# Moving the next chunk's first two gate steps between the transpositions of the first layer's chunks without fill

## The chip, the cores and the metric

The kernel runs on one core of one Trainium2 chip. The metric is the device time in microseconds of one launch, which covers all four layers of the network; the lower the better. A core has a matrix engine (TensorE, PE in the profile, with its weight loads as PEld), VectorE (DVE), ScalarE (ACT), GpSimd (POOL) and SyncE (SP, which here issues nearly all DMAs). Matrix products land in PSUM, from which VectorE and ScalarE copy them to SBUF.

## The reference

The input x has shape (8, 56, 56, 192). Four layers follow each other, each of the form x = x + layer(groupnorm(x)). Only layer 0, a gated convolution with Toeplitz matrices, is touched by the change:

```python
def _toeplitz(x, a):
    n = x.shape[1]
    m = 2 * n
    xf = jnp.fft.rfft(x, m, axis=1)
    af = jnp.fft.rfft(a, m, axis=0)
    return jnp.fft.irfft(xf * af[None], m, axis=1)[:, :n]
...
p = jax.nn.silu(x @ p_w.T + p_b)
q = jax.nn.silu(x @ q_w.T + q_b)
v = jax.nn.silu(x @ v_w.T + v_b)
...
qv = q * v
o1 = _toeplitz(qv.reshape(b * h, w, D1), a1).reshape(b, h, w, D1)
o2 = _toeplitz(jnp.transpose(qv, (0, 2, 1, 3)).reshape(b * w, h, D1), a2)
o2 = jnp.transpose(o2.reshape(b, w, h, D1), (0, 2, 1, 3))
out = p * (o1 + o2)
return out @ o_w.T + o_b
```

D1 is 576 channels, h and w are 56. a1 and a2 are small tables, one column per channel, computed once.

## The kernel before, in words

Layer 0 (`layer0`, from line 136) works image by image, b = 0 to 7, and within an image in five chunks c = 0 to 4 of its 576 channels. A chunk is two slabs of 64 channels (128 in all), but for the last, the tail, which is one slab. Everything is in 32-bit floats.

A chunk passes through three kinds of steps.

- **Gates and products** (`project`, line 283, four steps g = 0 to 3, each for a quarter of the image's rows). A step allocates PSUM tiles with `banks()` (tag "c", four slots of two banks each; a chunk of 128 channels needs two slots for q and v, the tail needs one), multiplies the normalized image by the weights on PE (L294 and L301), and evaluates SiLU twice on ScalarE into two SBUF tiles of the tag "s" (L310), of which there are four. `multiply` (line 316) then writes q times v into the one buffer `qv`, in two arrangements: a straight one on VectorE (L319) and a transposed one, mostly on GpSimd (L325, two instructions for each of g = 0 to 2; for g = 3 GpSimd and VectorE share it).
- **Turns** (`turn_both`, line 342, seven steps; `turn`, line 361, four steps for the tail). A step takes one PSUM slot, makes 16 transpositions of `qv` on PE (L352), and copies the result into the buffers ol and or (in the code `left` and `right`, for both slabs): the one half on VectorE, the other on ScalarE (L357). The copy on ScalarE begins when that on VectorE is done.
- **Convolutions** (`convolve`, line 382, two steps for a slab). A step takes one PSUM slot and makes 32 products of ol with or (L395), one channel each; the Toeplitz tables have been loaded by DMA into the other rows of ol and or. VectorE or ScalarE copies the result into `ot`. Behind a slab's last convolution `toeplitz` (line 265) has SP load the tables of the slab two further on, into the buffers that are free now. In image 0 these are built from small tables (`ed`) and stored to DRAM for the later images.

Every second chunk (c = 1 and 3) is followed by the output steps for two chunks (`post`, line 426): p, its SiLU (tag "s" too), transpositions of `ot`, products, and the output weights, added to `acca` and `accb`. The tail has the like in `post_tail`. They are kept as a list `fill` and run in the next chunk's turn phase.

The order of the work is written out in the loop from line 634. For a chunk c it is:

1. `merge(fill, turns)`: the chunk's turns, with the steps of `fill` in between. `fill` is the output of earlier chunks: of the tail of the image before for c = 0, of `post` for c = 2 and c = 4. It is empty for c = 1 and c = 3, and for c = 0 of image 0.
2. The next chunk's gates and products (`ahead`), merged with `beside`: in c = 0, 1 and 2 some steps of group norm (statistics of the image just finished, for the next layer, and the normalization of the next image). In c = 1 `beside` is `deviate` and `last` of `tell` (line 601), each with a small PE step (L98) between VectorE's.
3. The convolutions. In c = 3 (`c == NC - 2`) they alternate with the four tail gates of `ahead`.

`qv` exists once, so the next chunk's products must come behind this chunk's last turn, and the next chunk's turns behind all products.

TensorE's order is the order in which the code issues (line 627 puts PE under a manual schedule). The orders of the other engines are made by a planner that lists ready instructions by its own costs, earlier ones of the program first; the four slots of each tag are handed out in turn.

The merging rule spreads the shorter of two lists over the longer:

```python
def merge(a, b):
    n = max(len(a), len(b))
    for i in range(n):
        for x in (a, b):
            for f in x[-(-i * len(x) // n) : -(-(i + 1) * len(x) // n)]:
                f()
```

Of the kernel before, what the change touches and what calls it, by code (L numbers as in the profile page):

```python
# [73 lines left out]
def sub(ap, *dims):  # L74

    return bass.AP(ap.tensor, ap.offset, [list(ap.ap[0]), *(list(d) for d in dims)])
# [59 lines left out]
def layer0(cx, xin, xout, w, consts):  # L136
# [8 lines left out]
    NS, DS = 9, 64  # L145
# [5 lines left out]
    with ExitStack() as es:  # L151
# [7 lines left out]
        def banks():  # L159
            return cx.tile(psc, [128, 2, 512], "c")  # L160
# [104 lines left out]
        def toeplitz(n):  # L265

            b, s = divmod(n, NS)
            if b == B:
                return
            left, right = pairs[n % 2]  # L270
            sides = ((channels(right)[T2], T2), (channels(left)[T1], T1))
            if b:
                for d in (slice(d, d + 16) for d in range(0, DS, 16)):
                    for r, (dst, _) in enumerate(sides):
                        nc.sync.dma_start(dst[:, d], tables[s][r][:, d])
                return
            for r, (dst, _) in enumerate(sides):
                ed = eds[1 - r]
                src = bass.AP(ed.tensor, ed.offset + s * DS * NP, [[1, H], [NP, DS], [1, H]])
                nc.sync.dma_start(dst, src)  # L280
                nc.sync.dma_start(tables[s][r], dst)

        def project(xn, c):

            n = 7 * H
            tail = c == NC - 1
            js = [2 * c] if tail else [2 * c, 2 * c + 1]

            def step(g):
                pss = [banks() for _ in js]  # L290
                for j, ps in zip(js, pss):
                    for h in range(2):
                        at = h * HQ + g * n
                        nc.tensor.matmul(  # L294
                            ps[:, h, 0:n], wqv[0][:, j, :], xn[0][:, at : at + n],
                            start=True, stop=False,
                        )
                for j, ps in zip(js, pss):
                    for h in range(2):
                        rows = slice(h * CB, (h + 1) * CB)  # L300
                        nc.tensor.matmul(  # L301
                            ps[:, h, 0:n], wqv[1][rows, j, :], xn[1][rows, g * n : (g + 1) * n],
                            start=False, stop=True,
                        )
                ts = []
                for i in range(2):
                    j, ps = js[0 if tail else i], pss[0 if tail else i]
                    rows = slice(i * DS, (i + 1) * DS) if tail else slice(0, 128)
                    t = cx.tile(wk, [128, 2, n], "s")[0 : DS if tail else 128]
                    nc.scalar.activation(t, ps[rows, :, 0:n], AF.Silu, bias=bqv[rows, j : j + 1])  # L310
                    ts.append(t)
                multiply(g, slice(0, DS if tail else 128), ts)

            return [lambda g=g: step(g) for g in range(4)]

        def multiply(g, rows, ts):

            def straight():
                nc.vector.tensor_tensor(  # L319
                    sub(qv[rows, 7 * g :, 64 + H - 1 :], (HH * 120, 2), (120, 7), (-1, H)),  # L320
                    *(t.rearrange("p u (h w) -> p u h w", w=H) for t in ts), ALU.mult,
                )

            def across(eng, u, w0, w1):
                eng.tensor_tensor(  # L325
                    sub(qv[rows, w0:, H - 1 - 7 * g - HH * u :], (120, w1 - w0), (-1, 7)),
                    *(t[:, u].rearrange("p (h w) -> p w h", w=H)[:, w0:w1] for t in ts), ALU.mult,
                )

            if g < 3:  # L330
                straight()
                for u in range(2):
                    across(nc.gpsimd, u, 0, H)
                return

            for i, w in enumerate(((0, HH), (HH, H))):
                across(nc.gpsimd, 0, *w)
                across(nc.vector, 1, *w)
                if i == 0:
                    straight()  # L340

        def turn_both(n):

            order = (n % 2, 1 - n % 2)

            def step(i0):
                ps = banks()[0:120]
                view = ps.rearrange("p k (d i) -> p k d i", i=8)
                for i in range(8):
                    for e, k in enumerate(order):  # L350
                        rows = slice(e * DS, (e + 1) * DS)
                        nc.tensor.transpose(  # L352
                            view[:, k, :, i], qv[rows, i0 + i, :], ident[rows, rows]
                        )
                for t, rows, copy in zip(both, (T2, T1), (nc.vector.tensor_copy, nc.scalar.copy)):
                    dst = t[rows, :, 0:ND].rearrange("p k (d i) -> p k d i", i=H)
                    copy(dst[:, :, :, i0 : i0 + 8], view[rows])  # L357

            return [lambda i0=i0: step(i0) for i0 in range(0, H, 8)]

        def turn(n):

            s = n % NS
            e = s % 2 * DS
            left, right = pairs[n % 2]

            def step(i0, ni):
                ps = banks()[0:120]
                view = lambda k: ps[:, k].rearrange("p (d i) -> p d i", i=8)
                for i in range(ni):  # L370
                    nc.tensor.transpose(
                        view(i // 8)[:, :, i % 8], qv[e : e + DS, i0 + i, :],
                        ident[e : e + DS, e : e + DS],
                    )
                src = ps[:, 0 : ni // 8].rearrange("p k (d i) -> p d k i", i=8)
                for t, rows, copy in ((left, T2, nc.vector.tensor_copy), (right, T1, nc.scalar.copy)):
                    dst = channels(t)[rows, :, i0 : i0 + ni].rearrange("p d (k i) -> p d k i", i=8)
                    copy(dst, src[rows])

            return [lambda i0=i0: step(i0, min(16, H - i0)) for i0 in range(0, H, 16)]  # L380
# [233 lines left out]
# [7 lines that stand above are left out]
# [7 lines left out]
        xn, nxt = first, None  # L628
        merge(normalize(xn), [])
        for n in range(2):  # L630
            toeplitz(n)
        merge(project(xn, 0), [])
        fill, after, telling = [], None, []
        for b in range(B):
            more = b + 1 < B
            for c in range(NC):
                n = b * NS + 2 * c
                two = c < NC - 1
                turns = turn_both(n) if two else turn(n)
                merge(fill, turns)  # L640
                fill, beside = [], []
                if c == 0:
                    if after is not None:
                        image_dma(nc.sync, xout[b - 1], *after, store=True)
                        beside, telling = tell(b - 1, *after)
                    if more:
                        nxt = load_raw(b + 1)
                if c == 1:
                    acc = new_acc(b)
                    beside = [lambda f=f: f(bank) for f in telling]  # L650
                if c == 2 and more:
                    beside = normalize(nxt)

                if c % 2 == 0:
                    ot = cx.tile(cp, [120, 128, H] if two else [H, H, DS], "ot")
                ahead = project(xn, c + 1) if two else project(nxt, 0) if more else []
                convs = []
                for m in (n, n + 1) if two else (n,):
                    *some, last = convolve(m, ot)
                    convs += some + [lambda m=m, last=last: (last(), toeplitz(m + 2))]  # L660

                if c == NC - 2:
                    ahead = [f for pair in zip(ahead, convs[0:4]) for f in pair]
                    convs = convs[4:]
                merge(ahead, beside)
                for f in convs:
                    f()
                if c in (1, 3):
                    fill = post(c // 2, xn, ot, acc)
            fill, after = post_tail(xn, ot, acc), acc  # L670
            xn = nxt
# [1386 lines left out]
```

## Time and profile before

| | us |
|---|---|
| median of three runs | 4271.02 |
| lowest and highest of them | 4262.56, 4275.62 |
| the profiled execution's own time | 4265.11 |
| its span, first to last instruction | 4263.3 |
| granted TensorE clock, mean over the span | 0.971 |
| L352, matrix part: busy (3584 records) | 144.3 |
| L294, matrix part: busy (1152 records) | 435.9 |
| L310 on ACT: busy (320) | 278.2 |
| L357 on DVE and on ACT: busy (224 each) | 261.4 and 225.6 |
| L325 on POOL: busy (320) | 569.3 |

Times in the profile are microseconds from the first instruction of one execution. A line of the timeline reads: start, time busy, engine, source line, operation, tiles written and read, their sizes, and the number of instructions that were merged into the line; in brackets stands the idle time before it and what ended that. A matrix product in 32-bit floats can appear as more than one record, so the counts of L294, L301 and L395 are twice the code's. A line of the waits reads: engine, line, what it waited for, total, times, longest. A line of the stages reads: from and to, its length, then busy time and instructions of PE, PEld, DVE, ACT and POOL, the granted clock, the busy share of the DMA engines (slightly over 1 at times), and GB/s.

### The profile page before, as it was taken

What the parts mean: (1) busy time and instruction counts of PE and PEld (TensorE: products, weight loads), DVE (VectorE), ACT (ScalarE), POOL (GpSimd) and SP (SyncE); (2) the same over time, 40 slices, a digit from 0 to 9 for tenths busy, and PEclk for the clock granted to TensorE, in tenths of its full rate; (3) what the DMA queues carried; (4) which work ended last, traced back from release to release, by engine and by line L of the source; (5) the groups of instructions that cost most, each with busy time, mean ns of one, the idle gap of its engine ahead of it and who ended that gap; (6) DMA issues with size and microseconds to landing.
All of it is one profiled execution on the core that took longest, in us unless ns stands there. A gap on an engine that the chain in (4) does not pass through costs nothing.

```text
span 4263.3 us, 106441 instructions
## 1 busy us (share of the span) xinstructions
PE 3954.9 (93%) x46380; PEld 2553.1 (60%) x46380; DVE 2345.1 (55%) x3396; ACT 1781.1 (42%) x2020; POOL 1512.6 (35%) x1294
## 2 busy tenths in 40 slices
PE   6989999999999999999699999679998999998997
PEld 3666656666665656666366666434444555555997
DVE  4536565554656555464534444266666666664664
ACT  2434444334444433443233334133334555554664
POOL 3222232223223221332233333143334444444776
PEclk9999999999999999999799999889999999999999
DMA  6755242332524233241324444555547676664243
GB/s 142 141 106 145 62 114 71 81 86 62 145 62 115 74 81 84 62 122 47 92 75 107 97 105 108 146 153 169 166 141 186 167 166 162 151 156 112 73 115 94
DMA packets 379606, 484.13 MB, mean 114 GB/s; under 512 B 175780, under 2 KB 324372, under 8 KB 377236
## 3 DMA queue, kind: packets, MB, share of 16 engines
q1 hardware_dynamic: 373636, 466.97, 43.0%
q10 hardware_dynamic: 5504, 10.35, 0.8%
q8 instruction: 365, 5.98, 0.6%
q14 instruction: 101, 0.83, 0.1%
HBM read 321.49 MB, written 155.65 MB: 112 GB/s over the span
## 4 chain that ended last, share of the span: by engine, by line
PE 73%; DVE 7%; issue 7%; DMA 4%; SPq 3%; POOL 3%; ACT 2%; DVEq 0%; POOLq 0%; ACTq 0%
PE c L294 9%; PE v L1390 6%; PE c L395 6%; PE h L1892 5%; PE c L301 5%; PE c L481 4%; PE c L436 4%; PE c L943 4%; PE c L461 3%; PE y L978 3%; PE kv L1450 3%; PE c L443 3%; PE c L486 2%; DVE ol L357 2%; PE c L949 2%
## 5 line engine op out<-in xcount | busy, mean ns | idle before, releaser
L325 POOL TENSOR_TENSOR qv<-s,s 128x392 f32<-128x392 f32 (+3 forms) x320 | 569.3, 1799 | 1424.6 <-ACT s L310 1354.2
L294 PE MATMUL c<-xa,wqv 128*128 128x392 f32 x1152 | 435.9, 520 | 7.7 <-ACT or L357 4.8
L310 ACT ACTIVATE s<-c,bqv 128x784 f32<-128x784 f32 (+1 forms) x320 | 278.2, 910 | 389.9 <-PE c L301 232.8
L319 DVE TENSOR_TENSOR qv<-s,s 128x784 f32<-128x784 f32 (+1 forms) x160 | 190.4, 1190 | 268.2 <-ACT s L310 268.1
L357 ACT COPY or<-c 56x1024 f32<-56x1024 f32 x224 | 225.6, 1007 | 256.3 <-DVE ol L357 240.9
L294 PEld LDWEIGHTS c<-xa,wqv 128*128 128x128 f32 x1152 | 212.2, 196 | 177.2 <-issue 44.2
L395 PEld LDWEIGHTS c<-or,ol 120*64 120x64 f32 x9216 | 277.8, 138 | 55.7 <-issue 47.4
L395 PE MATMUL c<-or,ol 120*64 120x56 f32 x9216 | 287.2, 223 | 18.5 <-DMA ol<-ed 9.0
L357 DVE COPY ol<-c 56x1024 f32<-56x1024 f32 x224 | 261.4, 1208 | 63.4 <-PE c L352 63.4
L450 ACT ACTIVATE s<-c,bp 128x448 f32<-128x448 f32 x224 | 129.7, 630 | 271.0 <-PE c L443 271.0
L1390 PE MATMUL v<-wvb,wa 128*128 128x512 f32 (+1 forms) x400 | 192.6, 614 | 50.0 <-ACT wa L1301 30.7
L301 PE MATMUL c<-xb,wqv 64*128 64x392 f32 x1152 | 233.6, 519 | 0.0
L1923 POOL TENSOR_TENSOR y<-y,s 128x448 f32<-128x448 f32 x168 | 185.1, 1102 | 90.1 <-ACT s L1902 90.1
L1892 PE MATMUL h<-ringv,am 128*64 128x57 f32 (+1 forms) x4400 | 191.8, 235 | 18.3 <-DVE ringv L1879 11.3
L481 PE MATMUL c<-po,wo 128*128 128x448 f32 x448 | 198.1, 564 | 10.8 <-DVE po L470 10.8
L436 PE MATMUL c<-xa,wp 128*128 128x224 f32 x896 | 192.0, 358 | 3.2 <-issue 3.2
L1892 PE MATMUL h<-ringh,am 128*64 128x57 f32 (+1 forms) x4400 | 185.9, 231 | 8.0 <-DVE ringh L1898 7.8
L1401 ACT ACTIVATE vb<-sm 128x1024 f32<-128x1024 f32 (+1 forms) x100 | 103.7, 1038 | 211.2 <-issue 187.2
L424 DVE TENSOR_TENSOR acca<-c,acca 128x392 f32<-128x392 f32 (+1 forms) x120 | 67.3, 586 | 222.0 <-PE c L486 204.8
L352 PE MATMUL c<-ident,qv 64*120 64x64 f32 x3584 | 144.3, 227 | 44.2 <-ACT or L357 38.3
L1892 PEld LDWEIGHTS h<-ringv,am 128*64 128x64 f32 x4400 | 167.2, 140 | 21.5 <-DVE ringv L1879 12.2
L943 PE MATMUL c<-wv,xc 128*126 128x192 f32 x896 | 175.4, 339 | 0.7 <-DVE s L903 0.6
(224 smaller groups left out, 7690.6 us busy)
## 6 DMA issues: line engine op xcount, KB each, us to landing
or<-tt SPq DMA_DIRECT2D x252, 196.0 KB
ol<-tt SPq DMA_DIRECT2D x252, 196.0 KB
vt<-v SPq DMA_DIRECT2D x56, 672.0 KB
v<-vb SPq DMA_DIRECT2D x96, 384.0 KB
x<-x SPq DMA_DIRECT2D x112, 168.0 KB
x<-x SPq DMA_DIRECT2D x112, 112.0 KB
bt<-bs SPq DMA_DIRECT2D x28, 448.0 KB
bs<-bs SPq DMA_DIRECT2D x56, 224.0 KB
```

The lines of the kernel that those rows point to most:

```text
L294: nc.tensor.matmul(ps[:, h, 0:n], wqv[0][:, j, :], xn[0][:, at : at + n], start=True, stop=False,)
L301: nc.tensor.matmul(ps[:, h, 0:n], wqv[1][rows, j, :], xn[1][rows, g * n : (g + 1) * n], start=False, stop=True,)
L310: nc.scalar.activation(t, ps[rows, :, 0:n], AF.Silu, bias=bqv[rows, j : j + 1])
L319: nc.vector.tensor_tensor(sub(qv[rows, 7 * g :, 64 + H - 1 :], (HH * 120, 2), (120, 7), (-1, H)), *(t.rearrange("p u (h w) -> p u h w", w= ...
L325: eng.tensor_tensor(sub(qv[rows, w0:, H - 1 - 7 * g - HH * u :], (120, w1 - w0), (-1, 7)), *(t[:, u].rearrange("p (h w) -> p w h", w=H)[:, ...
L357: copy(dst[:, :, :, i0 : i0 + 8], view[rows])
L395: nc.tensor.matmul(ps[u * 64 : (u + 1) * 64, k, v * H : (v + 1) * H], left[:, d * H : d * H + 64], right[:, d * H : (d + 1) * H], start=Tr ...
L436: nc.tensor.matmul(out(u, h), wp[0][:, 2 * j + u, :], xn[0][:, at : at + n], start=(u == 0), stop=True, skip_group_check=True,)
L481: nc.tensor.matmul(pa, wo[:, 2 * j + u, 0:CA], pos[u], start=(u == 0), stop=(u == 1))
L943: nc.tensor.matmul(out(i, u), group(i, u), wv[0], start=(u == 0), stop=True, skip_group_check=True,)
L1390: nc.tensor.matmul(out, x[:, at : at + n], wt, start=(k == 0), stop=(k == 1), skip_group_check=True,)
L1892: nc.tensor.matmul(ps[sides[c], y], am[a][:, m * CB : (m + 1) * CB], old[:, x], start=(n < 2), stop=True, skip_group_check=True,)
```

## The change

`project` no longer returns four functions that each do gates and products, but four pairs: `gates(g)` (the matrix products and the SiLUs, whose two tiles are kept in a dictionary) and `products(g)` (the call of `multiply`). Where `fill` is empty, that is in c = 1 and c = 3 of all images and c = 0 of image 0, the first two gates of the next chunk take its place in the merge with the turns, and their two products are issued behind the last turn. By the merging rule the order on PE becomes gates 0, turns 0 to 2, gates 1, turns 3 to 6. The other two steps stay whole and where they were; in c = 1 they are merged with the two steps of `beside`, so that a small PE step of group norm stands behind each, and in c = 3 only the first two convolutions have gates ahead of them. In chunks with a fill nothing changes.

```diff
-            def step(g):
+            state = {}
+
+            def gates(g):
                 pss = [banks() for _ in js]
...
                     ts.append(t)
-                multiply(g, slice(0, DS if tail else 128), ts)
-
-            return [lambda g=g: step(g) for g in range(4)]
+                state[g] = ts
+
+            def products(g):
+                multiply(g, slice(0, DS if tail else 128), state.pop(g))
+
+            return [(lambda g=g: gates(g), lambda g=g: products(g)) for g in range(4)]
...
-        merge(project(xn, 0), [])
+        def whole(steps):
+            return [lambda f=f, h=h: (f(), h()) for f, h in steps]
+
+        merge(whole(project(xn, 0)), [])
...
                 turns = turn_both(n) if two else turn(n)
-                merge(fill, turns)
+
+                ahead = project(xn, c + 1) if two else project(nxt, 0) if more else []
+                early = [] if fill else ahead[0:2]
+                merge(fill + [f for f, _ in early], turns)
+                for _, f in early:
+                    f()
+                ahead = whole(ahead[len(early) :])
                 fill, beside = [], []
...
-                ahead = project(xn, c + 1) if two else project(nxt, 0) if more else []
...
                 if c == NC - 2:
-                    ahead = [f for pair in zip(ahead, convs[0:4]) for f in pair]
-                    convs = convs[4:]
+                    k = len(ahead)
+                    ahead = [f for pair in zip(ahead, convs[0:k]) for f in pair]
+                    convs = convs[k:]
                 merge(ahead, beside)
```

## Prediction

> **What bounds the kernel now.** I read the page first: its first part, for the engines' shares.
>
> ```profile
> PE 3954.9 (93%) x46380; PEld 2553.1 (60%) x46380; DVE 2345.1 (55%) x3396; ACT 1781.1 (42%) x2020; POOL 1512.6 (35%) x1294
> ```
>
> TensorE (PE) is busy for 93% of the span, so time can only be won where PE stands idle or runs at a lower clock, inside the first layer (about 48 to 2050 us of the span). Then I asked for PE's waits in that layer.
>
> ```profile
> PE c L352 <- ACT or L357: 38.3, 57, 1.6
> PE c L481 <- DVE po L470: 10.8, 16, 0.9
> PE c L395 <- DMA ol<-ed: 9.0, 1, 9.0
> PE c L294 <- ACT or L357: 4.8, 11, 0.4
> PE c L352 <- POOL qv L325: 2.5, 1, 2.5
> ```
>
> The columns are total us, times, longest. The largest wait that recurs is that of the transpositions (L352) for ScalarE's copy of an earlier one (L357). Next the order of time on PE in one chunk without fill, image 2, c = 1:
>
> ```profile
> 614.54 2.11 PE L352 MATMUL c<-ident,qv 64*120 64x64 f32 x64
> 617.58 0.69 PE L352 MATMUL c<-ident,qv 64*120 64x64 f32 x16 [0.93 <-ACT or L357]
> 618.72 0.68 PE L352 MATMUL c<-ident,qv 64*120 64x64 f32 x16 [0.45 <-ACT or L357]
> 619.85 1.11 PE L352 MATMUL c<-ident,qv 64*120 64x64 f32 x16 [0.45 <-ACT or L357]
> 620.98 3.92 PE L294 MATMUL c<-xa,wqv 128*128 128x392 f32 x8
> 624.83 1.59 PE L301 MATMUL c<-xb,wqv 64*128 64x392 f32 x8
> ```
>
> Four turns fill the four PSUM slots in 2.11 us (0.52 each); then each turn waits until a slot is copied out, at a pitch of 1.13 us. All engines in that stretch show why:
>
> ```profile
> 615.27 8.00 DVE L357 COPY ol<-c 56x1024 f32<-56x1024 f32 x7 [1.36 <-PE c L352]
> 616.52 7.80 ACT L357 COPY or<-c 56x1024 f32<-56x1024 f32 x7 [0.93 <-DVE ol L357]
> ```
>
> VectorE copies for 1.21 us, ScalarE 1.01 us after it: a slot is free again 0.21 + 1.21 + 0.03 + 1.01 + 0.05 = 2.5 us after its turn ends. The stages (busy us by engine, granted clock, DMA share, GB/s) of that stretch:
>
> ```profile
> 617.00:619.00 2.00, 0.97 (x24) 0.84 (x26) 2.00 (x3) 1.75 (x3) 0.00 (x0) 1.00 0.87 206
> 619.00:621.00 2.00, 1.53 (x31) 1.20 (x27) 2.00 (x3) 1.80 (x2) 0.00 (x0) 0.67 0.95 226
> 621.00:623.00 2.00, 2.00 (x3) 1.15 (x4) 2.00 (x3) 1.83 (x2) 0.00 (x0) 0.50 0.93 227
> ```
>
> PE is half idle at first, and the clock then falls to half while the first gates run (3.92 us for 2.90). Last, c = 3 of the same image:
>
> ```profile
> 725.42 2.10 PE L352 MATMUL c<-ident,qv 64*120 64x64 f32 x64
> ...
> 731.85 2.57 PE L294 MATMUL c<-xa,wqv 128*128 128x392 f32 x4 [0.45 <-ACT or L357]
> 734.35 1.59 PE L301 MATMUL c<-xb,wqv 64*128 64x392 f32 x4
> 735.87 2.08 PE L395 MATMUL c<-or,ol 120*64 120x56 f32 x64
> ...
> 738.03 3.98 POOL L325 TENSOR_TENSOR qv<-s,s 64x392 f32<-64x392 f32 x2 [14.25 <-PE c L395]
> ```
>
> **What the skill says.** The Trainium skill, "TensorE: Matmul & The Clock Gate", Part 1, says that the array's clock halves after a window of some 3.4 us with little activity, and Part 4 that transposes do not count as activity in the same way. The trace agrees in part: 0.67 and 0.50 after 5 us of turns here, but in five of the eight c = 1 stretches the gates run at 2.90 us, undisturbed. "PSUM — Partial Sum Buffer", Engine vs sequencer instructions, calls ScalarE's and VectorE's queues strict first in, first out; so a silu between two copies delays the later copies. "SBUF — State Buffer", Who interferes with whom, says that a VectorE instruction with two SBUF inputs contends with GpSimd's reads and one with at most one does not. L319 has two, the L357 copies none. The trace has GpSimd's L325 at 1.18 to 3.12 us for 0.91 to 2.35 us of L319, so contention is there, and the copies that GpSimd will now meet should not add to it.
>
> **The change, part by part.** It acts in 17 chunks: c = 1 and c = 3 of eight images and c = 0 of image 0. No arithmetic or DMA is added or removed. I count from a chunk's first PE instruction, with gates 4.35 us (593.89 to 598.24; in the tail chunk c = 3 2.38 us), their silus starting 3.9 us after the gates do (0.1 after their end in c = 3), 0.91 us each, turns 0.52 us.
>
> c = 1, before: from the first turn to the end of gates 0 the eight images show 11.75, 10.80, 11.81, 10.78, 11.09, 10.78, 12.47, 10.78 us; gates 1 and 2 add 8.70.
> c = 1, after: gates 0 to 4.35; turns 0 to 2 to 5.91; gates 1 need a slot freed by silu 0 (5.65) and that of turn 0 (7.35), and end at 10.3. Turn 3 ends at 10.82, its slot is free at 13.3; turns 4 to 6 end by 12.4. Gates 2 take that slot: idle 0.9, end 17.7. Against 10.78 + 8.70 = 19.5 that saves 1.8 us, more where the clock had fallen. Images 1 to 7: 78.5 + 60.9 - 7 x 17.7 = 15.5 us. One thing is given back: group norm's two small PE steps (L98) now have one gates step between them instead of two. The VectorE chain takes 3.6 us (627.26 to 630.86), the gates 4.35, but a product (0.97) may get in between: 0.3 us x 7 = 2. Net 13.5.
> In image 0 the second table (ol<-ed) lands 31.9 us after the first slab's convolutions release SP's queue (102.3 to 134.2), and its convolution starts at 134.7. A chunk 2.7 us shorter stalls for it: I keep 0.5.
>
> c = 3, before: 9.98, 9.83, 10.45, 9.82, 9.82, 9.83, 9.82, 10.13 us to the first convolution, then four convolutions of 2.0 and three gates of 2.38: 15.15.
> c = 3, after: gates 0 to 2.4, silus to 4.35, turns 0 to 2; ScalarE copies these till 7.6, then silus 1 till 9.45, then copies 3 to 6 till 13.5. ScalarE is now the bound: 7 copies and 4 silus are 7.1 + 3.6 = 10.7 us. PE does gates 1, turns 3 to 6 (the last at 9.5 to 10.0, on silu 1's slot) and gates 2 (10.5 to 12.9) meanwhile; the first convolution starts at 13.5, later than before, but with three gates done. Left are four convolutions and one gates: 10.15, end 23.65. Images 1 to 7: 69.7 + 7 x 15.15 - 7 x 23.65 = 10.2 us. In image 0 the table lands at 242.6 whatever PE does; only the gates that no longer follow that wait are won, 8.6 - 5.7 = 2.9.
>
> c = 0 of image 0, before: gates of chunk 0 end at 68.27, turns wait for GpSimd's qv until 70.88 and 72.97, gates 0 end at 85.41, gates 2 at 94.1. After: gates 0 fill 68.27 to 72.6, the wait is covered, gates 2 end near 86.3: 7.8 us.
>
> Products: GpSimd's pairs are 3.85 us, the last one 2.8, and now start at the last turn instead of after the silus. c = 1: 12.4 + 3 x 3.85 + 2.8 = 26.8 (with the silus' pace), wanted by the next turn at 23.85 + 7.6 + 2.75 = 34. c = 3: 10.1 + 14.4 = 24.5, wanted at 26.4. Hidden; without that cover each us late costs a us in a chunk. The four "s" tiles are all held by gates 0 and 1, so silus 2 wait for products 0 (16.7, wanted 17.2; c = 3: 13.95, wanted 13.5) and silus 3 for products 1 (20.0, wanted 21.6; c = 3: 17.8, wanted 18.1). Behind them on ScalarE stand only copies of convolutions, due 2 us later or more. SP's table loads are released at the ends of convolutions, as before; for b > 0 DMA goes quiet 10 to 15 us after the first turn, ahead of 13.5 and 23.9.
>
> Sum: 13.5 + 0.5 + 10.2 + 2.9 + 7.8 = 35 us. The profiled execution, 4265.11 us (span 4263.3), would become 4230; the median of the runs, 4271.02 (4262.56 to 4275.62), 4236. Unknown costs: the order that the planner gives ScalarE and VectorE (0 to 1 us a chunk, 17 us in all), and the clock: an idle 0.9 us beside 2 us of turns may still lower it, at 1.0 to 1.7 us each (the 11.81 and 12.47 above against 10.78), or its falls vanish, worth some 5 us more.
>
> **Rivals.** *ScalarE takes the gain back.* If silus and copies stand in a worse order, c = 3 gives nothing and c = 1 half: 35 - 13 - 7 = 15, 4256. For it: ScalarE has no idle time in c = 3; against: in the chunks with fill the same copies alternate with silus without idle PE. *GpSimd becomes the bound.* Its qv must be complete before the next chunk's turns; the margin in c = 3 is 1.9 us. If contention with VectorE brings each pair to twice the slowest single instruction seen (2 x 3.12 us) and the last to 3.5, c = 3 ends its products at 32.3, 5.9 late: 4.6 lost instead of 1.3 won, x 8 = 37 us; c = 1 loses 0.4 x 8 = 3. With the other gains (22) the net is +18: 4289. It costs from pairs of 4.5 us on and turns the sign near 5.6. Against: the pairs measure 3.8 to 4.0 with L319 beside them. *More than forecast*: no fall of the clock, c = 3 at PE's pace: 35 + 5 + 8 x 2 = 56, 4215. *It doesn't act*: PE's order is written by hand, so it must; I give that nothing.
>
> **How the numbers follow.** Forecast (4222 to 4250) 0.58; ScalarE (4250 to 4270) 0.22; GpSimd or another queue late 0.12, half of it beyond 4284; more 0.08. 0.3% (13 us) is about what a measurement tells from no change: faster, below 4258, is 0.58 + 0.08 + half of the ScalarE case's 0.22 = 0.77; I move 0.02 of it to slower, for a cost that I don't see: 0.75. Slower, beyond 4284, is 0.06 + 0.02 = 0.08; within, 0.11 + 0.06 = 0.17. The range 4212 to 4270 leaves out the GpSimd case and the far end of "more", some 0.16.
>
> **What would show it.** Right: L294 stands ahead of L352 in c = 1 and 3; L352's wait for ScalarE (38.3 us in total) falls to a third; convolutions of c = 3 start 13 to 14 us after the chunk does; the image period falls from about 249.5 us by 3. Wrong: L352 waits for POOL qv in c = 4 or 2 (GpSimd), L395 for ACT or L357 beyond 14 us (ScalarE), or a clock under 0.9 in these stretches.

## The result and the profile after

| | before | after |
|---|---|---|
| median of four runs, us | 4272.33 | 4227.9 |
| lowest and highest | 4262.56, 4275.62 | 4225.06, 4232.74 |
| ratio, with its 95% interval | | 0.9901 [0.9882, 0.992] |
| profiled execution: its own time, span | 4265.11, 4263.3 | 4228.55, 4226.7 |
| granted TensorE clock, mean over the span | 0.971 | 0.973 |

The forecast was 4236 us. In the changed file the lines below line 282 stand a few further down: the gates L294 and L301 are L297 and L304, the SiLU L310 is L313, the products L319 and L325 are L325 and L331, the transpositions L352 are L358, their copies L357 are L363, the convolutions L395 are L401 and the output weights' first product L436 is L442. The engines' shares, from the page's first part:

```profile
PE 3930.8 (93%) x46380; PEld 2546.5 (60%) x46380; DVE 2399.3 (57%) x3396; ACT 1780.1 (42%) x2020; POOL 1525.4 (36%) x1294
```

PE is busy with the same 46380 records for 24 us less, and idle for 12 us less. PE's waits in the first layer:

```profile
...
PE c L297 <- ACT or L363: 13.6, 17, 4.0
...
PE c L358 <- ACT or L363: 10.2, 9, 1.4
PE c L358 <- ACT s L313: 8.5, 8, 1.1
PE c L401 <- DMA ol<-ed: 8.4, 1, 8.4
...
PE c L401 <- issue: 4.8, 2, 3.9
PE c L98 <- DVE dev L124: 3.8, 7, 0.6
```

The transpositions' wait for ScalarE's copies has fallen from 38.3 to 10.2 us, and the wait for GpSimd's qv is gone from the list. In its place stand smaller waits at the new joints, of the gates for a copied slot (13.6) and of a transposition for the slot that a silu frees (8.5). "L98 <- DVE dev" is the price in group norm that the prediction put at 0.3 us an image: it is 0.54 (3.8 over 7).

The fall from 38.3 to 10.2 is not the net gain. All of PE's idle time in the layer that ends with ScalarE, copies and silus together, fell from 47.1 to 40.7 us (from 53.7 to 41.4 in a second pair of profiles, below). The larger part shows as busy time: the records of the transpositions take 136.5 us before and 121.1 after, since a turn that stands alone is shown with 0.68 us or more and turns in a row with 0.52 each.

PE in c = 1 of image 1, in order of time:

```profile
361.88 2.90 PE L297 MATMUL c<-xa,wqv 128*128 128x392 f32 x8
364.72 1.59 PE L304 MATMUL c<-xb,wqv 64*128 64x392 f32 x8
366.14 1.58 PE L358 MATMUL c<-ident,qv 64*120 64x64 f32 x48
367.65 3.06 PE L297 MATMUL c<-xa,wqv 128*128 128x392 f32 x8
370.64 1.59 PE L304 MATMUL c<-xb,wqv 64*128 64x392 f32 x8
372.06 2.10 PE L358 MATMUL c<-ident,qv 64*120 64x64 f32 x64
375.05 2.90 PE L297 MATMUL c<-xa,wqv 128*128 128x392 f32 x8 [0.89 <-ACT or L363]
```

Gates 0, three turns, gates 1, four turns without a gap. One wait is left: gates 2 begin 13.17 us into the chunk, after 0.89 us idle (the prediction had 13.3 and 0.9). The stages of this stretch in images 1 and 2:

```profile
361.88:379.39 17.51, 16.62 (x162) 9.97 (x160) 10.13 (x9) 11.41 (x12) 5.06 (x2) 1.00 0.75 183
605.45:622.95 17.50, 16.61 (x164) 9.96 (x160) 10.13 (x9) 11.41 (x12) 5.05 (x2) 1.00 0.72 185
```

PE is busy for 16.6 of 17.5 us and its clock is whole; so it is in the same stretch of all images from 1 to 7, where before it had fallen in some. The two starts are 243.57 us apart. From image 1 to image 7 the mean of this period is 244.1 us, and was 250.0 before: it fell by nearly 6 us, where the prediction's sign said 3.

c = 3 of image 1, PE first, then from all engines the silus that wait, and GpSimd:

```profile
468.69 1.58 PE L297 MATMUL c<-xa,wqv 128*128 128x392 f32 x4
...
473.16 1.58 PE L297 MATMUL c<-xa,wqv 128*128 128x392 f32 x4 [0.60 <-ACT s L313]
...
478.08 0.69 PE L358 MATMUL c<-ident,qv 64*120 64x64 f32 x16 [1.06 <-ACT s L313]
...
481.85 2.15 PE L401 MATMUL c<-or,ol 120*64 120x56 f32 x64 [0.30 <-ACT or L363]
```
```profile
483.06 1.85 ACT L313 ACTIVATE s<-c,bqv 64x784 f32<-64x784 f32 x2 [1.26 <-DVE qv L325]
486.71 0.91 ACT L313 ACTIVATE s<-c,bqv 64x784 f32<-64x784 f32 x1 [1.80 <-POOL qv L331]
```

The first convolution starts 13.16 us into the chunk (forecast 13.5), the last ends at 23.35 (23.65). Silus 2 and 3 wait for products, since gates 0 and 1 hold all "s" tiles; they start at 14.37 and 18.02 (forecast 13.95 and 17.8).

**Where the 36.6 us went.** I divide the first layer by image, and cut each image where a chunk's convolutions give way to output steps: the first stretch runs to the end of c = 1's convolutions, the second to the end of c = 3's, the third is the tail's. The third sums to 535.8 us before and after. By the first layer's end I mean the end of its last convolutions. It is at 2049.36 before and at 2006.44 after, 42.9 us sooner. The first stretches give 26.8 of these, the second 16.1. What comes after the first layer took 2213.9 us before and 2220.3 after. The change doesn't touch it: across the profiles of this study it took from 2207 to 2224, changed or not. So 42.9, and not the span's 36.6, is the better measure of the change in this execution.

### The profile page after: what moved, and what is told of

Read it like the earlier page. It is cut to its first block, busy times and chain, and to the rows that moved or that the text cites. A ratio compares the mean times of both kernels' runs of the same rounds, so it can differ in the third digit from the quotient of the medians.

```text
span 4226.7 us, 106475 instructions
## 1 busy us (share of the span) xinstructions
PE 3930.8 (93%) x46380; PEld 2546.5 (60%) x46380; DVE 2399.3 (57%) x3396; ACT 1780.1 (42%) x2020; POOL 1525.4 (36%) x1294
## 3 DMA queue, kind: packets, MB, share of 16 engines
q1 hardware_dynamic: 373636, 466.97, 43.9%
## 4 chain that ended last, share of the span: by engine, by line
PE 72%; DVE 9%; issue 5%; DMA 4%; SPq 4%; ACT 4%; POOL 2%; ACTq 0%; DVEq 0%; POOLq 0%
PE c L297 8%; PE v L1405 6%; PE c L401 6%; PE c L487 5%; PE c L442 4%; PE c L304 4%; PE h L1907 4%; PE c L958 4%; PE kv L1465 3%; PE y L993 3%; PE c L467 3%; PE c L449 3%; PE c L492 2%; PE c L1617 2%; PE c L964 2%
## 5 line engine op out<-in xcount | busy, mean ns | idle before, releaser
L331 POOL TENSOR_TENSOR qv<-s,s 128x392 f32<-128x392 f32 (+3 forms) x320 | 580.9, 1842 | 1368.8 <-ACT s L313 1137.5
L297 PE MATMUL c<-xa,wqv 128*128 128x392 f32 x1152 | 426.5, 511 | 21.3 <-ACT or L363 13.6
L313 ACT ACTIVATE s<-c,bqv 128x784 f32<-128x784 f32 (+1 forms) x320 | 278.7, 911 | 354.4 <-PE c L304 200.9
L363 DVE COPY ol<-c 56x1024 f32<-56x1024 f32 x224 | 262.9, 1210 | 138.0 <-PE c L358 138.0
L325 DVE TENSOR_TENSOR qv<-s,s 128x784 f32<-128x784 f32 (+1 forms) x160 | 247.0, 1555 | 150.4 <-ACT s L313 150.4
L363 ACT COPY or<-c 56x1024 f32<-56x1024 f32 x224 | 222.9, 1009 | 240.1 <-DVE ol L363 230.4
L297 PEld LDWEIGHTS c<-xa,wqv 128*128 128x128 f32 x1152 | 206.5, 191 | 184.8 <-issue 35.0
L401 PEld LDWEIGHTS c<-or,ol 120*64 120x64 f32 x9216 | 276.6, 139 | 39.0 <-issue 31.3
L401 PE MATMUL c<-or,ol 120*64 120x56 f32 x9216 | 283.2, 224 | 15.5 <-DMA ol<-ed 8.4
L304 PE MATMUL c<-xb,wqv 64*128 64x392 f32 x1152 | 232.9, 518 | 0.0
L1907 PE MATMUL h<-ringv,am 128*64 128x57 f32 (+1 forms) x4400 | 192.9, 235 | 20.4 <-DVE ringv L1894 13.3
L442 PE MATMUL c<-xa,wp 128*128 128x224 f32 x896 | 191.9, 357 | 0.0
L1434 POOL TENSOR_TENSOR l<-vb,ta 128x512 f32<-128x512 f32 (+1 forms) x52 | 73.1, 1406 | 287.5 <-ACT vb L1416 287.5
```

What stands on the lines that cost most here:

```text
L297: nc.tensor.matmul(ps[:, h, 0:n], wqv[0][:, j, :], xn[0][:, at : at + n], start=True, stop=False,)
L304: nc.tensor.matmul(ps[:, h, 0:n], wqv[1][rows, j, :], xn[1][rows, g * n : (g + 1) * n], start=False, stop=True,)
L325: nc.vector.tensor_tensor(sub(qv[rows, 7 * g :, 64 + H - 1 :], (HH * 120, 2), (120, 7), (-1, H)), *(t.rearrange("p u (h w) -> p u h w", w= ...
L331: eng.tensor_tensor(sub(qv[rows, w0:, H - 1 - 7 * g - HH * u :], (120, w1 - w0), (-1, 7)), *(t[:, u].rearrange("p (h w) -> p w h", w=H)[:, ...
L401: nc.tensor.matmul(ps[u * 64 : (u + 1) * 64, k, v * H : (v + 1) * H], left[:, d * H : d * H + 64], right[:, d * H : (d + 1) * H], start=Tr ...
L442: nc.tensor.matmul(out(u, h), wp[0][:, 2 * j + u, :], xn[0][:, at : at + n], start=(u == 0), stop=True, skip_group_check=True,)
```

## The experiments

**Theory.** A turn phase without fill moves at the pace of two engines' copies, and the gates between the turns are work that PE does in that time. **Rival A**: it isn't the alternation but any cover, or the mere order gates before turns, that wins. **Rival B**: GpSimd's products, now later, are near to being the bound. Three points arose from the traces: PE's idle time of the kind "issue" (no cause shown) fell from 13.1 to 4.8 us (the line "L401 <- issue" above), image 0 gained less than forecast, and PE's clock was higher.

### One half alone

In the first kernel c = 3 keeps the old order, in the second only c = 3 has the new one.

```diff
-                early = [] if fill else ahead[0:2]
+                early = [] if fill or c == NC - 2 else ahead[0:2]    # c = 1 and c = 0 alone
+                early = [] if fill or c < NC - 2 else ahead[0:2]     # c = 3 alone
```

> Early gates only in c = 1 (and in c = 0 of image 0); c = 3 as in the kernel before. Cover theory (gates fill PE's idle time between turns, chunk by chunk, and the chunks add up): the two traces put 26.8 us of the 42.9 us won in the first layer ahead of the end of c = 1, so about 4272 - 27 = 4245 us. Rival, that the gain comes mainly from c = 3, where the last convolutions no longer alternate with gates: 4265 us or more. If the two halves do not add up to the whole (this run and the next), something that they share made the gain.

> Early gates only in c = 3; c = 1 and c = 0 of image 0 as before. Cover theory: 16.1 us of the gain lay between the ends of c = 1 and c = 3, so about 4256 us. My forecast of the working alone was 13 us for this half (10.2 + 2.9): 4259. Rival that ScalarE, which has no idle time left in c = 3, takes it back: 4268 us or more.

c = 1 with image 0's c = 0: 4236.91 us (4236.31 to 4239.68; 4245 expected) against 4268.09, ratio 0.9926 [0.9904, 0.9948]; the first layer ends at 2017.42, 31.9 sooner than in the first profile of before. c = 3 alone: 4253.68 (4234.3 to 4258.46; 4256 expected), 0.9959 [0.9946, 0.9971]; the layer ends at 2033.85, 15.5 sooner. The halves sum to 47 us for 43 together, so they act nearly apart, each in the main in its own stretch: c = 1 alone takes 28.0 off the first stretches and 3.9 off the second ones, c = 3 alone 0.2 the wrong way and 15.7. The "issue" time is 3.1 us with the new order in c = 1, and 15.1 without.

### The same gates in front of the turns

Both gates stand ahead of turn 0: as much cover, no alternation.

```diff
-                merge(fill + [f for f, _ in early], turns)
+                for f, _ in early:
+                    f()
+                merge(fill, turns)
```

> The same two early gates and the same late products, but both gates stand in front of turn 0 and the seven turns follow undivided. Cover theory: the turns are alone again and PE waits for their copies as before, so c = 1 gains nothing, c = 3 some 0.2 us, and only the wait for qv in image 0 (about 4 us) is won: 4268 us (4258 to 4276), L358 waiting for ACT 35 to 45 us in total, and the clock falling in some of these stretches. Rival, that what helps is to have gates early (qv's products and silus sooner, fewer steps between turns and convolutions), wherever they stand: 4228 to 4240 us.

4241.8 us (4239.37 to 4256.94), ratio 0.9942 [0.9926, 0.9957]: the time is near what the rival said, not what my theory said. The waits of PE in the first layer tell why:

```profile
PE c L358 <- ACT or L363: 33.5, 60, 1.4
```

The transpositions wait for ScalarE as before (38.3 us then): here the theory held. The layer's gain of 23.7 us comes from elsewhere: 8.4 from image 0, where the gates cover the wait for GpSimd's qv and a table comes earlier; 10.6 from "issue" time (13.1 to 2.5); 4.7 from the rest, with 0.44 in most c = 3. In the first stretches of images 1 to 7, with the "issue" gaps taken off, it needs 551.5 us, and before needed 550.3: gates in front of the turns save nothing there. So rival A falls for the turn phases of c = 1. But it was right that the order alone wins something that my theory had not counted, and not little: 23.7 of the 42.9 us. Compared with this kernel, alternation wins 15.2 us more in c = 1 and 9.2 in c = 3 (images 1 to 7, gaps taken off), and is 4.8 us slower in image 0, in one profile of each.

### Turns first

In the changed kernel gates 0 stand ahead of turn 0, and gates 2 still wait 0.89 us. If three turns go first, their copies start earlier.

```diff
-                merge(fill + [f for f, _ in early], turns)
+                if early and n:
+                    (f0, _), (f1, _) = early
+                    turns = turns[0:3] + [f0] + turns[3:5] + [f1] + turns[5:]
+                    merge([], turns)
+                else:
+                    merge(fill + [f for f, _ in early], turns)
```

> Same change, other places in c = 1 and c = 3: turns 0 to 2, gates 0, turns 3 and 4, gates 1, turns 5 and 6 (c = 0 of image 0 as in the changed kernel). Cover theory: with two turns instead of four behind gates 1, gates 2 find the slots of turn 4 and silu 1 free sooner: c = 1 loses its last wait of 0.9 us, c = 3 starts its first convolution some 0.5 us earlier, so 4228 - 11 = 4217 us. Rival, that ScalarE's work or the copies of the last turn now set the end of the turn phase: 4224 to 4232 us, the wait only moving to L401 or to the gates in the middle.

4207.62 us (4204.66 to 4210.92), ratio 0.9856 [0.9834, 0.9879], the layer's end at 1987.75. That was better than I expected, so both kernels were run again beside each other on another chip, unchanged.

> The changed kernel once more, on the same chip as the next run. If the gain in the first layer is what the trace of the changed kernel shows, the layer ends at 2002 to 2010 us again, with 3 to 6 us put down to issue, and image 0 takes 136 us to the end of c = 1; if the 3.9 us gap in image 0 is chance, it is 132 to 134 there.

> The order turns 0 to 2, gates 0, turns 3 and 4, gates 1, turns 5 and 6 once more, beside the changed kernel on the same chip. If this order is truly better, 0.3 to 0.5% below the changed kernel (4206 to 4216 for 4228); if the first measurement of it owed its size to a lucky image 0 and to issue gaps, 4217 to 4228.

The changed kernel: 4223.65 (4217.41 to 4226.0), 0.99 [0.9878, 0.9923], the layer's end at 1999.96. Turns first: 4213.98 (4198.9 to 4216.02), 0.9868 [0.9843, 0.9893], end at 1989.8. The ratios' intervals overlap. The times themselves do not, and the layer ends 10 us sooner (19 between the first profiles of the two). PE in c = 1 of image 1 of turns first, second profile:

```profile
351.98 1.63 PE L358 MATMUL c<-ident,qv 64*120 64x64 f32 x48
353.55 3.06 PE L297 MATMUL c<-xa,wqv 128*128 128x392 f32 x8
...
364.29 2.90 PE L297 MATMUL c<-xa,wqv 128*128 128x392 f32 x8
```

Gates 2 begin 12.31 us into the chunk without a wait, 0.86 sooner than with gates first. In c = 3 the first convolution starts at 12.92 instead of 13.16. Over images 1 to 7, "issue" time taken off, the first stretches are 6 us shorter and the second 1.7.

### GpSimd's products longer

In the tail's step g = 0, GpSimd's two instructions are issued twice, which is work in c = 3 only. It was to eat 3.85 us of a margin that the prediction put at 1.9; in image 1 GpSimd's chain takes 17.89 us for 14.76, 3.1 more.

```diff
-                for u in range(2):
+                for u in (0, 1, 0, 1) if again else (0, 1):
...
-                multiply(g, slice(0, DS if tail else 128), state.pop(g))
+                multiply(g, slice(0, DS if tail else 128), state.pop(g), tail and g == 0)
```

> The changed kernel with GpSimd's two product instructions of step 0 issued twice in c = 3 alone (the same values are written again), so that its chain there is one pair, 3.85 us, longer. The forecast's step: the chain ends 1.9 us ahead of the next chunk's first turn (the trace of the changed kernel shows 0.9), so 8 x (3.85 - 1.9) = 16 to 8 x (3.85 - 0.9) = 24 us are lost: 4244 to 4252 us, and L377 (the tail's transpositions) waits for POOL qv. If silus 2 and 3, which wait for the products' tiles, are the tighter limit, more than 24. If GpSimd has far more room than reckoned: 4228 to 4234.

4229.28 us (4222.36 to 4239.46) against 4266.72, ratio 0.9916 [0.9893, 0.9938]. The second stretch grows by 1.7 to 2.2 us an image (98.23 to 99.94 in most), 12.6 us over images 1 to 7: less than the 16 to 24 expected, and the time itself, within 6 us of both medians of the changed kernel, lies where the expectation put GpSimd with far more room. The way it comes about isn't the expected one either. From all engines of c = 3 in image 1:

```profile
480.05 1.85 ACT L313 ACTIVATE s<-c,bqv 64x784 f32<-64x784 f32 x2 [5.00 <-POOL qv L331]
...
481.95 2.15 PE L401 MATMUL c<-or,ol 120*64 120x56 f32 x64 [0.32 <-ACT s L313]
...
485.02 2.08 PE L401 MATMUL c<-or,ol 120*64 120x56 f32 x64 [0.92 <-DVE ot L421]
```

No turn waits for qv. Silus 2 wait 5.00 us for GpSimd to release an "s" tile, where they waited 1.26 for VectorE before; VectorE's product waits for these silus, and its copy of a convolution (L421) stands behind that product, in the same queue. The convolutions then wait for their PSUM slot. The Trainium skill, "PSUM — Partial Sum Buffer", Engine vs sequencer instructions, calls such queues strict first in, first out; this trace agrees, with 0.92 us. So rival B is a real mechanism, with its first cost in the convolutions, and some 1.7 us for 3.1 of GpSimd's. It did not decide, because GpSimd's pairs stayed near their length: in c = 3 of the changed kernel five of its instructions take 10.12 us, 4.05 a pair, and the rival needed 4.5 to cost anything.

### What the "issue" gaps hang on

The kernel before once more; then with the two stores of normalization values put off to the end of c = 2's turns; then without the loads of the Toeplitz tables for images 1 to 7 (that part of the input is left out, so these images are computed with stale tables).

```diff
 # stores put off
-                nc.sync.dma_start(cx.norms[b][0:CA], nn[:, 0, :])
-                nc.sync.dma_start(cx.norms[b][CA:], nn[0:CB, 1, :])
+                def store():
+                    nc.sync.dma_start(cx.norms[b][0:CA], nn[:, 0, :])
+                    nc.sync.dma_start(cx.norms[b][CA:], nn[0:CB, 1, :])
...
+                if c == 2:
+                    while pending:
+                        pending.pop()()
 # loads left out
-            if b == B:
+            if b:
```

> The kernel before, profiled once more, unchanged. PE's idle time put down to issue (nothing waited for) was 13.1 us in its first layer, 8.5 of it in or right behind the convolutions of c = 1 in images 1 to 7, and 3 to 5 us in the kernels with early gates in c = 1. If these gaps belong to the order of the instructions, they come again at the same places with 9 to 16 us; if they are chance, they stand elsewhere or are few, and the first layer ends up to 10 us sooner than at 2049.

> The kernel before, with the two small DMAs that store an image's group norm values (8 bytes to a packet) issued after the turns of c = 2 instead of beside the convolutions of c = 1. Theory that PE's instructions arrive late because that store holds the DMA engines just when convolutions use up instructions fastest: the 8.5 us of issue gaps in c = 1 fall below 2, the first layer ends 6 to 9 us sooner than at 2049, 4260 to 4264 us. Rival, that the table loads or the order of PE's work alone make the gaps: they stay at 7 to 10 us, 4268 us.

> The kernel before without the loads of the Toeplitz tables in images 1 to 7 (left out: these images are convolved with whatever tables stand in the buffers). The issue gaps within the turns of images 1 to 7 (0.47, 0.76 and 1.25 us, 2.5 in all), which fall together with table loads at a DMA share of 0.9, go away if the loads cause them; those of the convolutions stay at 7 to 10 us if the norm store or the order causes them, and fall below 3 if the loads do.

Before again: 4264.93 us in its one run, the layer's end at 2043.81, "issue" time 12.7 us, again 14 gaps, six of them ahead of the very same instruction as in the first profile. Here is one in the first profile of before, then the same in the second, ahead of two records of a convolution in image 3:

```profile
899.84 0.32 PE L395 MATMUL c<-or,ol 120*64 120x56 f32 x2 [1.67 <-issue]
```
```profile
894.12 0.32 PE L395 MATMUL c<-or,ol 120*64 120x56 f32 x2 [2.13 <-issue]
```

They are no mere chance, then. With the stores put off: 4266.55 (4257.74 to 4278.86), ratio 1.0001 [0.999, 1.0012], "issue" 16.0: the idea that this pair of DMAs holds PE's instructions up falls. Without the loads: 4271.25 in its one run, "issue" 10.6, all of it ahead of convolutions:

```profile
PE c L395 <- issue: 10.6, 9, 3.5
```

The gaps ahead of transpositions (3.0 us in the first profile of before) are gone in this one profile, those ahead of convolutions remain. In images 1 to 7 the gaps in the first stretches are 7.1 to 13.7 us in all five profiles that have the old order in c = 1, and 0 to 1.2 in all seven that have gates ahead of or between its turns, gates in front and turns first included. The gaps hang on the order of PE's instructions there, whatever the waits.

The traces say what PE waits for. The page has a DMA queue of the kind "instruction":

```profile
q8 instruction: 365, 5.98, 0.6%
```

Its 365 packets have 16384 bytes each, and the trace of before has 93467 records on PE's queue, 256 to a packet. Over the first layer of all twelve profiles there are 93 "issue" gaps, 83.9 us in sum. 79 of them (75.3 us) stand where a count of these records in steps of 256 begins anew (193 or 194 over a multiple of 256, but for one at 192), and all but one of the 79 end 1.22 to 1.88 us after such a packet has landed. For the gap of 1.67 us above, a packet lands at 898.29 and PE goes on at 899.84. In no profile does PE start a block of 256 in this layer sooner than 1.22 us after the packet's end. So these gaps are PE waiting for its own instructions, and no DMA of the kernel's data is what it waits for. What makes a packet late (some took over 3 us for a median of 1.1, others started late), and why early gates avoid it, no run shows.

## Why the prediction was right, and where not

The sum by the prediction's own steps, against two pairs of profiles (first: before and after; second: before again and after again). The gaps are those of the kind "issue"; in image 0 they are not split off.

| us won | forecast | first pair | second pair |
|---|---|---|---|
| c = 1, images 1 to 7, gaps taken off | 13.5 | 14.1 | 13.7 |
| c = 1, gaps | not in the sum | 8.9 | 10.1 |
| c = 3, images 1 to 7, gaps taken off | 10.2 | 14.7 | 12.4 |
| c = 3, gaps | not in the sum | 1.6 | 1.5 |
| image 0 | 11.2 | 3.6 | 6.2 |
| sum | 35 | 42.9 | 43.9 |

**Right: the mechanism and the schedule, of some three quarters of the gain.** The largest recurring wait was that of turns for copies, and alternation takes it: gates in front don't (33.5 us of it left), gates between do (10.2, with part of the wait moved to gates and silus). The schedule counted by hand from durations of before was within 0.5 us at each point looked at: gates 2 at 13.17 for 13.3, convolutions of c = 3 at 13.16 for 13.5, their end at 23.35 for 23.65, silus 2 and 3 at 14.37 and 18.02 for 13.95 and 17.8. c = 1 came out as forecast. That the whole sum, 35, came near 43 is partly luck: the gaps, 10.5 and 11.6 us, have no term in it, and image 0 gave 7.6 and 5.0 less than forecast.

**Mis-sized: image 0, by losses that had no term.** c = 0 did what was said: gates 2 begin at 80.8 and end at 85.2, for 86.3 forecast, and the first convolutions start 9.0 us sooner (6.7 in the second pair). Much of this is lost again in c = 1. The planner put statistics of the next image on VectorE ahead of the copies of c = 1's later turns, and gates 2 wait for these. From all engines of the changed kernel:

```profile
108.73 1.02 DVE L115 BATCH_NORM_STATS2 st<-xb 128x6 f32<-128x392 f32 x2
...
111.65 4.60 DVE L363 COPY ol<-c 56x1024 f32<-56x1024 f32 x4
113.95 4.43 PE L297 MATMUL c<-xa,wqv 128*128 128x392 f32 x8 [4.01 <-ACT or L363]
```

This recurs in the second profile (4.00 us). The prediction named the planner's order as an unknown of 0 to 1 us a chunk; here it is 4. The kernel with turns first has no such stall. In the first pair a gap of 3.89 us (1.31 before) and 2.3 us of lower clock in the output steps follow; in the second pair neither does. So the convolutions of c = 2's first slab end only 1.5 us sooner (3.3 in the second pair). Then c = 3 waits for a table:

```profile
242.68 3.67 PE L395 MATMUL c<-or,ol 120*64 120x56 f32 x64 [8.99 <-DMA ol<-ed]
```
```profile
241.32 6.41 PE L401 MATMUL c<-or,ol 120*64 120x56 f32 x128 [8.36 <-DMA ol<-ed]
```

The prediction said that this table lands "whatever PE does". That is wrong: SP issues the tables of c = 3 one after the other when c = 2's first slab has been convolved, and in all twelve profiles PE goes on 29.1 to 31.9 us after the end of that slab (31.5 and 31.7 in the first pair, 30.6 and 29.5 in the second). It is the chain that the prediction had counted rightly in c = 1 (31.9). What is won ahead of the release moves the landing with it; what is won between the release and the landing is waited away. The landing comes 1.36 and 4.39 us sooner, and gates that no longer follow the wait give 2.3 and 1.8 (2.9 forecast): 3.6 and 6.2 in all.

**Mis-sized: c = 3.** 1.70 us an image where the clock was whole (99.93 to 98.23) for 1.33 forecast, 11.9 over seven. The rest, 0.5 to 2.8, stands in single images of before, most of it in two of the first profile (1.5 and 1.0 us) in whose second stretch the clock had fallen. The forecast's own figure for that, "some 5 us more" over both kinds of chunk, was left out of the sum. One minus the clock, integrated from 60 to 2000 us, is 35.8 and 20.5 us in the two profiles of before, 18.8 and 11.9 in those of the changed kernel; so much differs from one execution to the next that only the direction is shown.

**Not seen: the gaps.** PE's idle time of the kind "issue" has no term in the prediction's sum: it was left where it was without a reason, and this is the step that failed. The trace of before held it (in the first layer 13.1 us in total, in pieces of 0.3 to 3.2). The new order removes 10 of them. They alone are larger than the difference of the forecast from the result.

**The rivals.** ScalarE took nothing back: in images 1 to 7 no convolution of c = 3 was late. GpSimd was not the bound, and with 3.1 us more on it, it cost 1.7 to 2.2 us per tail chunk, by another way than the rival's: through the "s" tiles and VectorE's queue. L98's share came to 3.8 us for a forecast of 2.

**Better than both kernels** is turns first, 1.1 to 1.7% below the kernel before by its two intervals, and some 0.2% below the changed one where both ran beside each other. Some 8 us of its gain on the changed one lie in images 1 to 7. **Left open**: what makes a block of PE's instructions late, and why early gates avoid it; and why the table loads of image 0 take 29 us in one execution and 32 in another.

## What to carry to other kernels

- When one engine waits at the pace of two others' copies, put its independent work between the waiting steps, not in front of them; and let a few of the waiting steps go first, so that the copies start at once.
- A schedule counted by hand from the durations of the profile before was good to half a microsecond in repeated chunks. It was weak in the first image, where a load's landing decides. Ask there what starts the load: what is won ahead of its start moves the landing, what is won after it is waited away.
- Idle time without a cause in the profile is a term of the sum too. If it recurs at the same instructions in a second profile, a new order can remove it, or bring it. Look at the queue that carries the engine's own instructions.

## What the runs showed of the hardware

PE can wait for its own instructions: they come in packets of 16384 bytes, one for 256 records, and PE never began a block sooner than 1.22 us after its packet had landed (all twelve profiles, first layer). Waits at the start of a block cost 10.9 and 10.5 us in the layer in the two profiles of before, 4.8 and 1.2 in those of the changed kernel.

VectorE's straight products (L319, in the changed file L325) take 247.0 us instead of 190.4 for the same 160 instructions, a mean of 1555 ns for 1190, while GpSimd's 320 instructions go from 569.3 to 580.9 only. From the page's groups:

```profile
L325 DVE TENSOR_TENSOR qv<-s,s 128x784 f32<-128x784 f32 (+1 forms) x160 | 247.0, 1555 | 150.4 <-ACT s L313 150.4
```

The two ran side by side before as well. What changed is which starts first. In steps g = 0 to 2 a VectorE product takes 0.91 to 0.98 us when no GpSimd product is running at its start, and up to 2.39 when one is; that holds for 26 of 120 before and for 76 after. A GpSimd product takes 1.60 us in the mean alone and 2.32 when a VectorE product is running at its start (means of before; 106 times of 240 before, 104 after). So in the main the later one pays. I had expected GpSimd to suffer more; VectorE took nearly all of the increase, and had the time to spare.
